# Causal masks moved to TensorE and probability sums shared by two engines in a two-layer attention kernel

## Chip, cores and metric

The kernel runs on one core of a Trainium2 chip. The metric is the device time of one execution in microseconds (us), smaller is better. The engines have short names in the profile: PE is TensorE (matmuls), PEld its weight loads, DVE VectorE, ACT ScalarE, POOL GpSimd, SP SyncE (here it only issues DMAs).

## The reference

The program is two transformer layers over 2048 tokens of width 512. Layer 0 is linear attention plus a mixture of 16 experts, layer 1 is softmax attention in a causal window of 1024 tokens (16 heads of 32) plus a block on the 256 tokens that a router picks. The change touches one piece of layer 1 alone, the softmax attention:

```python
scores = jnp.einsum('bhqd,bhkd->bhqk', q, k) / np.sqrt(HD)
scores = jnp.where(mask[None, None, :, :], scores, NEG)
attn = jax.nn.softmax(scores, axis=-1)
out = jnp.einsum('bhqk,bhkd->bhqd', attn, v)
```

with `mask = (q_idx >= k_idx) & (q_idx - k_idx <= 1024)` over n = 2048 tokens. A query sees itself and the 1024 tokens ahead of it, so in tiles of 128 tokens a query tile needs at most nine key tiles. The first of the nine (the edge of the window) and the last (the diagonal) are half masked.

## The kernel before

**Two passes over the scores.** The kernel computes the scores twice. The first pass (`maxima`, line 498) has queries on the partitions and finds the largest score of each query and head; it adds its masks on PE, as matmuls of a bf16 identity with a bf16 mask (`ident_b`, `mask_b`, lines 520 to 526). The negated maxima are kept transposed in `negT`, in two bf16 halves. This pass runs piece by piece between other work and ends at about 1462 us.

The second pass is the last stage of the program, from line 1054 on. It has the keys on the partitions, so that the exponentials can go into the next matmul without a transpose. It goes by *groups* (Q, g): Q is a block of four query tiles (512 queries), g a set of four heads. Each group goes by *units* (`units`, line 1077). A unit is one key tile against the query tiles of the block that see it. Key tiles seen by all four query tiles make whole units. Those at the edge of the window see only the first one, two or three query tiles, and are joined with the diagonal ones, which see the rest, so that such a unit has two key tiles and is full too. Q 0 has four units, the last three of them shorter (384, 256 and 128 queries); Q 1 has eight, the last three short in the same way; Q 2 and Q 3 have nine full ones. The order of the groups is written out in lines 1230 and 1231: (2,0), (0,0), (2,1), (0,1) and so on to (0,3), then (1,0) to (1,3), then (3,0) to (3,3).

**What a unit does.** `probabilities` (line 1093) takes two tiles of score buffers in PSUM from `ps_s` (three buffers, each two heads by 512 queries). PE writes the scores of the four heads side by side, each in its own 32 rows of the array (line 1104), and adds the negated maxima with a matmul over two rows (line 1111). Where the unit touches the edge or the diagonal, VectorE adds the mask `maskT` in PSUM (line 1128), once for each half (two heads). ScalarE then takes the exponential of each half (line 1137) into SBUF. The first unit of a group writes its exponentials into `acc`, the accumulator of the group; the others write to `pt`, a ring of six buffers, that is three units.

**Values and sums.** One step later PE multiplies the probabilities by the values (`values`, line 1169; the matmul is line 1177) into the PSUM tile `av`. The softmax also needs the sum of the probabilities over all keys. `gathered` (line 1197) does this in one of two ways. Either PE multiplies the unit's probabilities by a block of ones into the PSUM tile `sm` (`sums`, line 1186; matmul in line 1191), or the unit is added elementwise to `acc` (line 1210), by GpSimd, or, for unit 2 of the groups with Q > 0, by VectorE. `summed` (line 1162) chooses: PE takes the full units with even number except 0 and 2. There is one `sm` tile only, for all groups in turn.

**The end of a group.** `ending` (line 1212) is a generator of which one piece is run after each step of the next group. Its first piece only waits. The second has PE sum `acc` into `sm`, and VectorE take the reciprocal of two of its four blocks of 128 queries (line 1219) and multiply the values in `aT` by it (line 1220). The third does the other two blocks. With the last set of heads (g = 3) four pieces follow, each of which multiplies one query tile by `w_out` and adds the residual (`output`, line 1141). What is left of an ending when the next group is over is run at once.

**The loop** (line 1233) emits, for each unit: its scores, mask and exponential; then values and sums of the unit before; then one piece of the ending. Each engine works through its own queue in that order and waits by semaphores where it needs another one's result or a free buffer.

Of the kernel before, what the change touches and what calls it, by code (L numbers as in the profile page):

```python
# [19 lines left out]
P = 128  # L20
# [18 lines left out]
def two_layer_kernel(ctx: ExitStack, tc: tile.TileContext, a: dict, out: bass.AP):  # L39
# [6 lines left out]
    def const(shape, name, pool=cpool, dtype=F32):  # L46
        return pool.tile(shape, dtype, tag=name, name=name)
# [55 lines left out]
    def vcopy(o, i):  # L103
        V.tensor_copy(o, i)
# [354 lines left out]

    mask = const([P, 3, P], "mask", l1)  # L460
    maskT = const([P, 2, P], "maskT", l1)
    mask_b = const([P, 3, P], "mask_b", l1, BF16)
    for m in (mask, maskT):
        G.memset(m, 0.0)
    for m, step, mult in (
# [4 lines left out]
            channel_multiplier=mult,  # L470
        )
    vcopy(mask_b, mask)
    ones_b = const([P, P], "ones_b", l1, BF16)
    G.memset(ones_b, 1.0)
    ones_f = const([P, HD], "ones_f", l1)
# [590 lines left out]
        )  # L1066
    w_out = const([P, NC, D], "w_out", vo_pool)
    load(nc.sync, w_out, a["w_out"].rearrange("(c p) o -> p c o", p=P))
    pt = ctx.enter_context(tc.tile_pool(name="pt", bufs=6, reuse_waits="tile"))
    acc_pool = ctx.enter_context(tc.tile_pool(name="acc_pool", bufs=2, reuse_waits="tile"))  # L1070
    wk = ctx.enter_context(tc.tile_pool(name="wk7", bufs=2, reuse_waits="tile"))
    ps_s = ctx.enter_context(tc.tile_pool(name="ps_s", bufs=3, **tight))
# [20 lines left out]
    def probabilities(g, unit, name, base):  # L1093


        q0, q1 = unit[0][1] * P, (unit[-1][2] + 1) * P
        n = q1 - q0
        pS = [
            ps_s.tile([P, 2, QT * P], F32, tag="s", name=f"ps_{name}_{hp}") for hp in range(2)
        ]  # L1100
        for m, (kb, t0, t1) in enumerate(unit):
            for h in range(4):
                r = slice(h * HD, (h + 1) * HD)
                PE.matmul(  # L1104
                    pS[h // 2][:, h % 2, t0 * P - q0 : (t1 + 1) * P - q0],
                    kT[r, g, kb * P : (kb + 1) * P], qT[r, g, t0 * P : (t1 + 1) * P],
                    start=m == 0, stop=False, skip_group_check=True,
                )
        for h in range(4):
            r = slice(h * HD, h * HD + 2)  # L1110
            PE.matmul(  # L1111
                pS[h // 2][:, h % 2, :n], ones_b[r, :], negT[r, g, q0:q1], start=False, stop=True,
                skip_group_check=True,
            )
        edge = unit[0][2] == unit[0][0] + NWB - 1
        causal = unit[-1][1] == unit[-1][0]
        spots = []
        if edge and causal and len(unit) == 2:
            spots = [(unit[0][2], 0, 2)]
        else:  # L1120
            spots += [(unit[0][2], 0, 1)] if edge else []
            spots += [(unit[-1][1], 1, 2)] if causal else []
        got = []
        for hp in range(2):
            for tile_, m0, m1 in spots:
                s = slice(tile_ * P - q0, tile_ * P - q0 + (m1 - m0) * P)
                w = (m1 - m0) * P
                V.tensor_tensor(  # L1128
                    pS[hp][:, :, s], pS[hp][:, :, s],
                    maskT[:, m0:m1, :].rearrange("p m k -> p (m k)").unsqueeze(1)  # L1130
                    .to_broadcast([P, 2, w]), ALU.add,
                )
            if base:
                pT = acc_pool.tile([P, 2, QT * P], F32, tag=f"acc{hp}", name=f"acc_{name}_{hp}")
            else:
                pT = pt.tile([P, 2, QT * P], F32, tag="pt", name=f"pt_{name}_{hp}")
            S.activation(pT[:, :, :n], pS[hp][:, :, :n], AF.Exp)  # L1137
            got.append(pT)
        return got
# [14 lines left out]
    class Group:  # L1154
# [7 lines left out]
        def summed(self, n):  # L1162


            if (self.Q, self.g) == (NT // QT - 1, NC - 1) and n == len(self.us) - 2:
                return True
            return n % 2 == 0 and n != 2 and self.us[n][-1][2] - self.us[n][0][1] == QT - 1

        def values(self, n, got):
            Q, g, unit = self.Q, self.g, self.us[n]  # L1170
# [26 lines left out]
        def gathered(self, n, got):  # L1197

            unit, o = self.us[n], QT * self.Q * P
            q0, q1 = unit[0][1] * P - o, (unit[-1][2] + 1) * P - o  # L1200
            if n == 0:
                self.acc = got
            elif self.summed(n):
                self.sums(got, q0, q1, False)
            else:

                eng = V if n == 2 and self.Q > 0 else G
                for hp in range(2):
                    part = self.acc[hp][:, :, q0:q1]
                    eng.tensor_tensor(part, part, got[hp][:, :, : q1 - q0], ALU.add)  # L1210

        def ending(self):

            Q, g, aT = self.Q, self.g, self.aT
            yield
            self.sums(self.acc, 0, QT * P, True)
            for j in range(QT):
                js = slice(j * P, (j + 1) * P)
                V.reciprocal(self.sm[:, js], self.sm[:, js])  # L1219
                V.tensor_tensor(aT[:, g, js], aT[:, g, js], self.sm[:, js], ALU.mult)  # L1220
                if j % 2:
                    yield
            if g == NC - 1:
                for j in range(QT):
                    output(QT * Q + j, aT, j * P)
                    yield
# [79 lines left out]
```

## Time and profile before

| what | value |
|---|---|
| median of three timed runs | 1873.57 us (1873.55 to 1880.08) |
| the profiled execution, its own time | 1869.43 us |
| its span, from the first instruction to the last | 1867.7 us |
| granted TensorE clock, mean | 0.970 of full speed |
| second score pass, first score matmul to last sum | 1463.3 to 1849.9 us |
| score steps in it | 120, 72 of them with a mask |
| mask adds on VectorE (line 1128) | 144, 68.3 us busy |
| adds to acc (line 1210) | 126 on GpSimd, 253.8 us; 24 on VectorE |
| exponentials (line 1137) | 240, of which 208 to pt: 182.2 us |
| matmuls of sums (line 1191) | 360, of which 232 for single units |

A row of the page's fifth part, or of an answer by line, names the line, engine and operation, what it writes and reads with its shape, how often, the busy time, the mean of one in ns, and the idle time of the engine just ahead of it with what ended it. A float32 matmul shows as two instructions, so one unit of four heads shows as eight. In a table of windows the columns are start and end, length, the busy time and number of instructions of PE, PEld, DVE, ACT and POOL, then the granted clock, the DMA share and GB/s. A line of a timeline has the start in us, the time to the end of the last of a run of like instructions, engine, line, operation and number; in brackets the idle time ahead of it. Matmuls are pipelined, so how long a piece of PE's work takes is read from the start of one run of matmuls to the start of the next, not from the ends.

### The profile page before, as it was taken

The page shows a single profiled execution, that of the slowest core. Times are in us where ns is not written, and L with a number is a line of the kernel's source. Part 1 is how long each engine was busy: PE and PEld are TensorE (multiplying, and loading weights), DVE is VectorE, ACT ScalarE, POOL GpSimd, SP SyncE. Part 2 cuts the span into 40 slices and gives each one's busy share as a digit, 9 for nine tenths or more (in the row PEclk, how much of TensorE's full clock was granted, in tenths as well). Part 3 has the DMA queues.
Part 4 walks back from the last instruction along what each step waited for, and adds up shares of the span by engine and source line. Part 5 has one row for each costly group of instructions (what it writes and reads, how often), then busy time and mean ns, then how long its engine had stood idle before and what let it go on. Part 6 is the DMA issues. An engine that isn't in the chain of part 4 may idle for free. (4 is left out here: it accounts for less than half of the span.)

```text
span 1867.7 us, 20604 instructions
## 1 busy us (share of the span) xinstructions
PE 1740.5 (93%) x8120; PEld 767.4 (41%) x8120; DVE 1008.1 (54%) x1445; ACT 573.7 (31%) x923; POOL 497.2 (27%) x372
## 2 busy tenths in 40 slices
PE   7999999999999999868988887999999999999999
PEld 4555444344444333323433333454565333333333
DVE  6775645436445343696666564575555455444344
ACT  3212334233233243111111111142100366446463
POOL 2110000100100110333344431331000467458583
PEclk9999999999999999989999897999999899999999
DMA  9301001210213130100001004311132300110100
GB/s 362 128 29 43 23 28 39 85 34 29 72 53 74 33 109 23 62 23 23 23 23 29 26 12 149 122 51 68 46 111 92 91 1 1 35 57 1 46 1 35
DMA packets 61810, 107.12 MB, mean 57 GB/s; under 512 B 12209, under 2 KB 13745, under 8 KB 61201
## 3 DMA queue, kind: packets, MB, share of 16 engines
q1 hardware_dynamic: 55280, 104.01, 16.7%
q0 software_dynamic: 1152, 1.21, 0.4%
q8 instruction: 63, 1.03, 0.2%
q10 hardware_dynamic: 5280, 0.59, 0.2%
q14 instruction: 35, 0.28, 0.0%
HBM read 84.14 MB, written 21.65 MB: 57 GB/s over the span
## 5 line engine op out<-in xcount | busy, mean ns | idle before, releaser
L527 DVE TENSOR_REDUCE mx<-pa 128x4 f32<-128x1536 f32 (+3 forms) x144 | 252.9, 1756 | 178.2 <-PE pa L523 83.8
L1210 POOL TENSOR_TENSOR acc<-acc,pt 128x1024 f32<-128x1024 f32 (+3 forms) x126 | 253.8, 2047 | 122.1 <-ACT pt L1137 75.8
L1137 ACT ACTIVATE pt<-ps 128x1024 f32<-128x1024 f32 (+3 forms) x208 | 182.2, 923 | 138.1 <-DVE ps L1128 86.4
L515 PE MATMUL pa<-kT,qT 32*128 32x384 f32 (+3 forms) x1152 | 158.0, 562 | 47.5 <-DVE mx L527 39.3
L1104 PE MATMUL ps<-qT,kT 32*128 32x512 f32 (+3 forms) x1152 | 162.0, 535 | 8.6 <-ACT pt L1137 8.1
L93 POOL TENSOR_TENSOR xr<-xr,xn 128x512 f32<-128x512 f32 x16 | 27.0, 1697 | 493.6 <-DVE xn L87 493.6
L424 PE MATMUL acc<-h,rw2T 128*128 128x512 f32 x256 | 135.3, 616 | 14.9 <-DVE h L290 14.3
L288 ACT ACTIVATE r_e<-eg 128x512 f32<-128x512 f32 x128 | 75.8, 594 | 222.4 <-PE eg L419 202.4
L782 PE MATMUL p<-w_qk,xnt 128*128 128x512 f32 x256 | 129.7, 631 | 8.3 <-ACT xnt L107 8.3
L290 DVE TENSOR_TENSOR h<-ea,r_e 128x512 f32<-128x512 f32 x128 | 87.0, 686 | 87.2 <-ACT r_e L289 59.9
L421 PE MATMUL ea<-xw,rw1T 128*128 128x512 f32 x256 | 130.7, 592 | 0.0
L419 PE MATMUL eg<-xl,rwgT 128*128 128x512 f32 x256 | 130.7, 592 | 0.0
L1128 DVE TENSOR_TENSOR ps<-ps,maskT 128x256 f32<-128x256 f32 (+1 forms) x144 | 68.3, 514 | 100.3 <-PE ps L1111 97.2
L1104 PEld LDWEIGHTS ps<-qT,kT 32*128 32x128 f32 x1152 | 62.2, 186 | 116.5 <-issue 55.4
L515 PEld LDWEIGHTS pa<-kT,qT 32*128 32x128 f32 x1152 | 52.0, 191 | 138.3 <-DVE mx L527 88.0
L1177 PE MATMUL av<-pt,v 128*32 128x512 f32 (+3 forms) x1024 | 102.3, 485 | 0.2
L415 DVE TENSOR_TENSOR xw<-xw,xl 128x512 f32<-128x512 f32 x64 | 43.9, 685 | 94.9 <-DMA xw<-w_d 94.9
L1219 DVE RECIPROCAL sm<-sm 128x128 f32<-128x128 f32 x64 | 61.8, 965 | 57.4 <-PE sm L1191 56.0
L424 PEld LDWEIGHTS acc<-h,rw2T 128*128 128x128 f32 x256 | 43.4, 188 | 95.5 <-DVE h L290 79.4
L289 ACT ACTIVATE r_e<-r_e 128x512 f32<-128x512 f32 x128 | 80.2, 629 | 6.4 <-issue 1.9
L650 POOL TENSOR_TENSOR t<-qk,cosg 128x1024 f32<-128x1024 f32 x15 | 35.3, 2354 | 161.7 <-DVE qk L645 145.5
L421 PEld LDWEIGHTS ea<-xw,rw1T 128*128 128x128 f32 x256 | 48.6, 190 | 61.2 <-issue 60.8
(278 smaller groups left out, 2542.2 us busy)
## 6 DMA issues: line engine op xcount, KB each, us to landing
xw<-w_d SPq DMA_DIRECT2D x64, 256.0 KB, 3.2
x<-in_x SPq DMA_DIRECT2D x16, 256.0 KB, 4.3
res_d<-x SPq DMA_DIRECT2D x16, 256.0 KB, 2.3
xr<-res_d SPq DMA_DIRECT2D x16, 256.0 KB, 4.8
xn_d<-xn SPq DMA_DIRECT2D x16, 256.0 KB, 2.4
res_d<-xr SPq DMA_DIRECT2D x16, 256.0 KB, 2.0
xnq<-xn_d SPq DMA_DIRECT2D x16, 256.0 KB, 2.9
v_d<-vt SPq DMA_DIRECT2D x16, 256.0 KB, 2.9
```

Source lines behind the costliest of these rows:

```text
L289: S.activation(r, r, AF.Square)
L290: V.tensor_tensor(dst, pa, r, ALU.mult)
L419: PE.matmul(pg, rwgT[:, e, hb], xl, start=True, stop=True)
L421: PE.matmul(pa, rw1T[:, e, hb], xw, start=True, stop=True)
L424: PE.matmul(acc, rw2T[:, j, e, :], h, start=e == 0 and j == 0, stop=e == E - 1 and j == 1,)
L515: PE.matmul(pS[:, h, : w * P], qT[r, g, i * P : (i + 1) * P], kT[r, g, ks], start=True, stop=not (edge or last),)
L527: V.tensor_reduce(mx[:, g, :, c], pS[:, :, : w * P], AX.X, ALU.max)
L782: PE.matmul(pj, xnt[:, c, :], w, start=c == 0, stop=c == NC - 1)
L1104: PE.matmul(pS[h // 2][:, h % 2, t0 * P - q0 : (t1 + 1) * P - q0], kT[r, g, kb * P : (kb + 1) * P], qT[r, g, t0 * P : (t1 + 1) * P], start ...
L1137: S.activation(pT[:, :, :n], pS[hp][:, :, :n], AF.Exp)
L1177: PE.matmul(self.av[h * HD : (h + 1) * HD, t0 * P - o : (t1 + 1) * P - o], vs[kb // 4][:, kb % 4, hs], got[h // 2][:, h % 2, t0 * P - q0 : ...
L1210: eng.tensor_tensor(part, part, got[hp][:, :, : q1 - q0], ALU.add)
```

## The change

Three things change, all in the second pass.

The masks of this pass are added by PE: a bf16 copy `maskT_b` of `maskT` is made once, and after the matmul of the negated maxima four matmuls per masked unit, one for each head, add `ident_b` times the mask into the scores. VectorE's 144 adds in PSUM are gone. A mask matmul has 128 columns where one mask applies, 256 where the unit joins edge and diagonal.

Of each group at most one unit is summed on PE (13 in all, 29 before): none for Q 0, unit 4 for Q 1, the last unit for Q 2 and Q 3, and as before also the last but one of the very last group. All other units are added to `acc`, the odd ones by GpSimd and the even ones by VectorE: 110 adds on GpSimd and 72 on VectorE.

The `pt` ring has eight buffers instead of six, and for groups with Q > 0 the ending begins after three idle pieces instead of one, so that the sums of `acc` are emitted in the fourth step of the next group. What is left of it when a Q 0 group is over (the second half of the divisions, and for (2,3) all four outputs) is emitted in one run in the first step of the group after.

The order of the instructions of ScalarE and SyncE is the same as before. On PE, VectorE and GpSimd nothing differs ahead of this pass except the one cast that makes `maskT_b`.

```diff
--- before.py
+++ after.py
@@ -459,6 +459,7 @@
 
     mask = const([P, 3, P], "mask", l1)
     maskT = const([P, 2, P], "maskT", l1)
+    maskT_b = const([P, 2, P], "maskT_b", l1, BF16)
     mask_b = const([P, 3, P], "mask_b", l1, BF16)
     for m in (mask, maskT):
         G.memset(m, 0.0)
@@ -470,6 +471,7 @@
             channel_multiplier=mult,
         )
     vcopy(mask_b, mask)
+    vcopy(maskT_b, maskT)
     ones_b = const([P, P], "ones_b", l1, BF16)
     G.memset(ones_b, 1.0)
     ones_f = const([P, HD], "ones_f", l1)
@@ -1066,7 +1068,7 @@
         )
     w_out = const([P, NC, D], "w_out", vo_pool)
     load(nc.sync, w_out, a["w_out"].rearrange("(c p) o -> p c o", p=P))
-    pt = ctx.enter_context(tc.tile_pool(name="pt", bufs=6, reuse_waits="tile"))
+    pt = ctx.enter_context(tc.tile_pool(name="pt", bufs=8, reuse_waits="tile"))
     acc_pool = ctx.enter_context(tc.tile_pool(name="acc_pool", bufs=2, reuse_waits="tile"))
     wk = ctx.enter_context(tc.tile_pool(name="wk7", bufs=2, reuse_waits="tile"))
     ps_s = ctx.enter_context(tc.tile_pool(name="ps_s", bufs=3, **tight))
@@ -1106,12 +1108,6 @@
                     kT[r, g, kb * P : (kb + 1) * P], qT[r, g, t0 * P : (t1 + 1) * P],
                     start=m == 0, stop=False, skip_group_check=True,
                 )
-        for h in range(4):
-            r = slice(h * HD, h * HD + 2)
-            PE.matmul(
-                pS[h // 2][:, h % 2, :n], ones_b[r, :], negT[r, g, q0:q1], start=False, stop=True,
-                skip_group_check=True,
-            )
         edge = unit[0][2] == unit[0][0] + NWB - 1
         causal = unit[-1][1] == unit[-1][0]
         spots = []
@@ -1120,16 +1116,23 @@
         else:
             spots += [(unit[0][2], 0, 1)] if edge else []
             spots += [(unit[-1][1], 1, 2)] if causal else []
+        for h in range(4):
+            r = slice(h * HD, h * HD + 2)
+            PE.matmul(
+                pS[h // 2][:, h % 2, :n], ones_b[r, :], negT[r, g, q0:q1], start=False,
+                stop=not spots, skip_group_check=True,
+            )
+
+        for m, (tile_, m0, m1) in enumerate(spots):
+            s = slice(tile_ * P - q0, tile_ * P - q0 + (m1 - m0) * P)
+            for h in range(4):
+                PE.matmul(
+                    pS[h // 2][:, h % 2, s], ident_b,
+                    maskT_b[:, m0:m1, :].rearrange("p m k -> p (m k)"), start=False,
+                    stop=m == len(spots) - 1, skip_group_check=True,
+                )
         got = []
         for hp in range(2):
-            for tile_, m0, m1 in spots:
-                s = slice(tile_ * P - q0, tile_ * P - q0 + (m1 - m0) * P)
-                w = (m1 - m0) * P
-                V.tensor_tensor(
-                    pS[hp][:, :, s], pS[hp][:, :, s],
-                    maskT[:, m0:m1, :].rearrange("p m k -> p (m k)").unsqueeze(1)
-                    .to_broadcast([P, 2, w]), ALU.add,
-                )
             if base:
                 pT = acc_pool.tile([P, 2, QT * P], F32, tag=f"acc{hp}", name=f"acc_{name}_{hp}")
             else:
@@ -1164,7 +1167,7 @@
 
             if (self.Q, self.g) == (NT // QT - 1, NC - 1) and n == len(self.us) - 2:
                 return True
-            return n % 2 == 0 and n != 2 and self.us[n][-1][2] - self.us[n][0][1] == QT - 1
+            return n == {0: -1, 1: 4}.get(self.Q, len(self.us) - 1)
 
         def values(self, n, got):
             Q, g, unit = self.Q, self.g, self.us[n]
@@ -1204,7 +1207,7 @@
                 self.sums(got, q0, q1, False)
             else:
 
-                eng = V if n == 2 and self.Q > 0 else G
+                eng = G if n % 2 else V
                 for hp in range(2):
                     part = self.acc[hp][:, :, q0:q1]
                     eng.tensor_tensor(part, part, got[hp][:, :, : q1 - q0], ALU.add)
@@ -1212,7 +1215,8 @@
         def ending(self):
 
             Q, g, aT = self.Q, self.g, self.aT
-            yield
+            for _ in range(3 if Q > 0 else 1):
+                yield
             self.sums(self.acc, 0, QT * P, True)
             for j in range(QT):
                 js = slice(j * P, (j + 1) * P)
```

## The prediction

> **What bounds the kernel now.** I read the page first, then the table of windows for the second score pass (first score matmul at 1463.3 us, last probability sum at 1849.9 us), then TensorE's timeline inside it, then the groups of line 1210, at last the waits.
>
> ```profile
> PE 1740.5 (93%) x8120; PEld 767.4 (41%) x8120; DVE 1008.1 (54%) x1445; ACT 573.7 (31%) x923; POOL 497.2 (27%) x372
> L1128 DVE TENSOR_TENSOR ps<-ps,maskT 128x256 f32<-128x256 f32 (+1 forms) x144 | 68.3, 514 | 100.3 <-PE ps L1111 97.2
> ...
> 1463.00:1850.00 387.00, 377.90 (x3245) 132.15 (x3246) 175.87 (x301) 220.91 (x257) 255.42 (x127) 0.97 0.09 28
> ```
>
> In the pass PE is busy 377.9 of 387 us, VectorE 175.9, ScalarE 220.9, GpSimd 255.4. But a "busy" PE may be one whose matmuls are stretched by a wait, so I go by the starts:
>
> ```profile
> 1436.36 0.40 PE L523 MATMUL pa<-mask_b,ident_b 128*128 128x128 bf16 x4
> 1436.59 1.08 PE L1035 MATMUL pm<-wd,act 128*128 128x512 f32 x2
> ...
> 1772.94 1.14 PE L1104 MATMUL ps<-qT,kT 32*128 32x512 f32 x8
> 1773.90 0.40 PE L1111 MATMUL ps<-negT,ones_b 2*128 2x512 bf16 x4
> 1774.23 1.07 PE L1177 MATMUL av<-pt,v 128*32 128x512 f32 x8
> 1775.23 1.36 PE L1104 MATMUL ps<-qT,kT 32*128 32x512 f32 x8
> ...
> 1781.53 1.07 PE L1177 MATMUL av<-pt,v 128*32 128x512 f32 x8
> 1782.41 1.04 PE L1191 MATMUL sm<-pt,ones_f 128*32 128x512 f32 x8
> 1783.38 1.15 PE L1104 MATMUL ps<-qT,kT 32*128 32x128 f32 x16
> ```
>
> A step without a wait is 0.96 (scores) + 0.33 (maxima) + 1.00 (values) = 2.29 us. A unit summed on PE makes it 0.85 longer (values and sums take 1.85 here, 1781.53 to 1783.38). Four mask matmuls of 128 columns in the first pass cost 0.23 (1436.36 to 1436.59).
>
> The pair of groups (Q 2, then Q 0) from 1503.28 to 1540.54 took 37.26 us. Its floor: nine steps of 2.29 for Q 2, for Q 0 by the same reading 2.29, 1.84, 1.33 and 0.86, and five sums: 20.6 + 6.3 + 4.25 = 31.2. So PE waits 6.1 us in a pair, mostly where VectorE's mask stands between scores and exponential. A Q 3 group takes 26.4 us, 2.5 of them waits; a Q 1 group 20.6 in the mean of three.
>
> Last, who adds probabilities:
>
> ```profile
> L1210 POOL TENSOR_TENSOR acc<-acc,pt x126: 724/2356/3426, 1471.5 to 1840.4; 128x1024 f32<-128x1024 f32 x78, 128x768 f32<-128x768 f32 x16, 128x512 f32<-128x512 f32 x16, 128x256 f32<-128x256 f32 x16
> L1210 DVE TENSOR_TENSOR acc<-acc,pt x24: 1206/1215/2232, 1475.0 to 1832.4; 128x1024 f32<-128x1024 f32 x24
> ...
> 1799.60 0.97 DVE L1219 RECIPROCAL sm<-sm 128x128 f32<-128x128 f32 x1 [4.39 <-PE sm L1191]
> 1801.00 0.97 DVE L1219 RECIPROCAL sm<-sm 128x128 f32<-128x128 f32 x1
> ```
>
> A GpSimd add takes 2.36 us, a VectorE add 1.21, but the longest are 3.43 and 2.23: each time the two met, the later one was longer by what was left of the other. The recip and multiply of one 128-column block take 1.33, four of them 5.3 us.
>
> [...] the masks (one operand in PSUM) ran beside GpSimd without loss, 0.70 at most. [...] The trace is divided: values followed by sums take 0.88, followed by scores 1.00, so about 0.11 for a change; scores followed by full-array masks in the first pass show none (1435.50 to 1436.36 is two passes of 0.43).
>
> **The change part by part.** Against the profiled execution: span 1867.7, its own time 1869.4, which is 0.2% under the 1873.6 median.
>
> *PE.* Of the 29 units summed on PE 13 stay: 16 x 0.85 = 13.6 us less. Masks: 48 units get four matmuls of 128 columns at 0.23 = 11.0; 24 get four of 256. No row shows these[...]. PE gets 8.0 us more work. Bounds: [...] nothing comes off, since the matmuls must run.
>
> *VectorE.* 144 masks go (68.3 us), 48 adds come: 72 instead of 24, of them 32 more of 1.21 and 16 of half the elements, estimated at 0.65, 49 us in all. Its sum falls little; its place changes: no mask is left between scores and exponential. What then sets PE's waits is the score buffer (three, two used per unit): the exponential of the first half ends 0.16 + 0.97 us after the scores, and PE has 1.00 of values to do meanwhile, so 0.1 a step remains, and 0.64 after the first step of Q 2 or Q 1, whose values are short. The one cast of the mask (about 0.3 us, near 775 us) lies in front of a 1.6 us idle stretch of VectorE: nothing.
>
> *A pair for PE alone.* 26.9 + 3 x 0.85 + masks (two of 0.23, three of 0.44, four of 0.23 in Q 0: 2.7) + 0.64 + 0.3 = 33.1 instead of 37.26.
>
> *The new wait.* The sums of a group now come three steps into the next, and both groups share the one PSUM tile sm. Q 0's sums (second step of the next Q 2) wait until VectorE has divided Q 2's; those divisions stand in its queue behind the add of Q 0's unit 2; that waits for GpSimd's unit 1; that for the end of Q 2's chain of adds, in which every link now is serial[...]. Round the loop, from one pair's Q 0 sums to the next: sums 0.97 + start 0.1 + divisions 5.3, then V, G, V, G, V, G for units 2 to 7 (V pair 2.2, from 1476.12 to 1478.33[...]; G pair 4.6) 20.4, G of unit 1 of Q 0 with 768 elements 3.55, V 1.2, divisions 5.3: 36.8 us. Longer than PE's 33.1, so the pair takes 36.8. The first pair (40.0 before, at a lower clock) has no divisions in front and saves 4.1. Its chain starts 8.2 in, where GpSimd's first add is now: 8.2 + 4.6 + 20.4 + 3.55 + 1.2 + 5.3 = 43.2, and PE asks for sm at 35.9 + 4.7 = 40.6. It waits 2.6, so the second pair saves 1.5, the other two 0.5 each: 6.6.
>
> *The outputs of Q 2* now go out in one run at the start of Q 1, behind the same divisions. Counted from the last pair's start, without its wait, V ends at 36.1 and the first block is divided at 37.4; PE is there at 33.1 + 1.9 = 35.0 and waits 2.4. Q 1's first group, whose waits are hidden under outputs now, has 0.9 of masks: together -3.3.
>
> *Q 1, groups 1 to 3.* PE alone 19.0 (15.5 of steps, two sums, 0.9 masks, 0.9 waits). Unit 4's sums need sm, whose divisions stand behind V of unit 2, and that behind G of unit 1. From the group's start: unit 1's first half is ready at 4.9, + 0.1 + 4.6 + 2.2 + 5.3 = 17.1; PE is there at 14.9 (six steps of 1.9, 2.9, 2.35, 3.2, 2.35 and 2.2). So 21.2 instead of 20.6: -1.8.
>
> *Q 3.* PE: 20.6 + two sums 1.7 + masks 1.8 + waits 0.2 = 24.3. The chain of adds takes 4 x 4.6 + 3 x 2.2 + 0.7 (V of unit 4 behind divisions) = 25.7, but its sum is wanted 10 us into the next group only, so for three groups PE's time counts. Saved: 0.9 (first, 25.2 without its outputs), 2.05 and 2.2. In the last one the chain starts 2.8 late and nothing follows that hides it: its sums wait 2.4, and 0.6 is left of 3.0. Together +5.75.
>
> Sum: 6.6 - 3.3 - 1.8 + 5.75 = 7.2 us, 0.4%. The buffers (eight) carry a chain that is up to four units late; with six, ScalarE would wait.
>
> **Rivals.** *The chain doesn't bind* (divisions start earlier, adds overlap more): PE alone sets the time. Then 4 x 4.1 - 0.9 + 3 x 1.6 + 8.15 = 28.4: 1845. For it: PE is 93% busy, and GpSimd's adds stood 75.8 us waiting for exponentials, which then come sooner. Against: the loop's links are all measured.
> *Every change of hands costs more.* GpSimd and VectorE will hand the accumulator over six times in a Q 2 or Q 3 group, where it is twice in the kernel before, so the trace shows few handovers, and no loss in them. The loop has nine such links. At 0.5 us each a pair takes 41.3: the third and fourth pairs then lose 4 each, the second 1.4, the outputs behind 2.5 more, each Q 1 group 1.0 more, and in Q 3 the chain (29.4) sets the pace: -5.3 - 5.8 - 4.8 - 6 = -22. In between it goes in a line: it turns the gain into a loss from 0.13, a measurable one from 0.29. At 0.3 it is -10: 1884.
> *The masks on PE cost more than 0.23 and 0.44* moves the forecast by up to 7.9, less where the loop hides it.
>
> **How the numbers follow.** What tells from no change is about 0.5%, 9.4 us. Forecast 0.45: 1873.6 - 7.2 = 1866 (1862.2 in the profiled execution), own range 1858 to 1875. Chain not binding 0.33, handovers 0.22. Faster: 0.33 and the forecast's lower edge 0.07 = 0.40; slower: most of the handover case, 0.20; the rest 0.40. The range for 8 in 10 takes in both rivals' centres: 1846 to 1885.
>
> **What would show it.** Right: waits of PE's sums for VectorE's multiply of 2 to 4 us at each Q 2 after the first and each Q 1 after the first; VectorE adds with a mean near 2 us[...]; pairs of some 36.8 us. Wrong: pairs near 33 us (first rival), GpSimd pairs much over 4.7 us with idle gaps at each handover (second), or mask matmuls that take more than 0.44 for four.

## The result, and the profile after

The changed kernel takes 1862.1 us in the median of 19 runs (1855.7 to 1870.8), the kernel before 1873.6 beside it on the same chip (1868.9 to 1880.1): a ratio of 0.9943, 95% interval 0.9930 to 0.9957, so by the ratio 10.7 us less (8.1 to 13.1; the two medians are 11.4 apart). The profiled execution spans 1853.8 us.

From the page of the kernel after, the engines' totals and the groups of the additions and exponentials (busy us, mean ns of one, idle us just before them and what ended most of it); then, from the table of windows, the second score pass (engines in the order PE, PEld, DVE, ACT, POOL, then the granted clock, the DMA share and GB/s):

```profile
PE 1728.1 (93%) x8280; PEld 772.6 (42%) x8280; DVE 1039.0 (56%) x1350; ACT 572.5 (31%) x923; POOL 490.7 (26%) x356
...
L1213 POOL TENSOR_TENSOR acc<-acc,pt 128x1024 f32<-128x1024 f32 (+2 forms) x110 | 246.8, 2267 | 125.8 <-ACT pt L1140 62.6
L1140 ACT ACTIVATE pt<-ps 128x1024 f32<-128x1024 f32 (+3 forms) x208 | 181.1, 923 | 131.4 <-PE ps L1129 74.2
...
L1213 DVE TENSOR_TENSOR acc<-acc,pt 128x1024 f32<-128x1024 f32 (+1 forms) x72 | 124.6, 1760 | 129.1 <-POOL acc L1213 104.3
```

```profile
1456.00:1836.00 380.00, 369.30 (x3405) 137.91 (x3405) 204.77 (x205) 219.87 (x257) 248.38 (x111) 0.98 0.09 29
```

The row of masks on VectorE is gone, and the exponentials now wait for PE's mask matmuls (L1129). VectorE's 72 additions take 124.6 us, where alone they would cost some 79 (56 of 1.21 us and 16 of 0.68, what those of each shape take that wait for nothing; the 49 of the prediction are for the 48 that come): their mean is 1.76 us, and 104.3 us of VectorE's idle time ended with a GpSimd addition. VectorE and GpSimd work on one chain, one after the other.

The second score pass, from the start of the first score matmul to the start of the last probability sum, is 386.1 us before and 379.0 after. The groups of the two profiles, each from the start of its first exponential to that of the next group's, worked out from the traces, with three of the experiments below beside them:

| Stretch | before | masks alone | change | Q 0 on GpSimd | + Q 1's sums early |
|---|---|---|---|---|---|
| first pair (Q 2 and Q 0) | 39.5 | 38.3 | 36.8 | 36.7 | 36.8 |
| second pair | 37.3 | 36.3 | 35.7 | 35.1 | 35.1 |
| third pair | 37.3 | 36.1 | 36.6 | 35.1 | 35.1 |
| fourth Q 2 | 26.3 | 26.1 | 28.2 | 25.2 | 25.2 |
| fourth Q 0, and Q 1's first group with outputs | 60.3 | 57.2 | 57.1 | 57.1 | 57.1 |
| Q 1, three groups | 61.8 | 60.7 | 66.5 | 68.1 | 59.1 |
| Q 3, first group with outputs | 40.2 | 41.2 | 38.9 | 38.9 | 38.7 |
| Q 3, the other three | 80.9 | 81.9 | 77.0 | 77.0 | 77.0 |

So the change gains 3.0 us in the pairs (the fourth Q 2 with them), 3.2 around the outputs of Q 2 and 5.3 in Q 3, and loses 4.7 in Q 1; with 0.3 ahead of the first exponential that is the 7.1 in all. The fourth Q 0, which the forecast counts with the pairs, stands with the outputs here. The pass starts 6.9 us earlier as well, in code that the change hardly touches.

TensorE's timeline of the change shows the price of a mask. The columns are start, length of the group, engine, line, output and inputs, tile, shape and count:

```profile
1776.29 1.15 PE L1106 MATMUL ps<-qT,kT 32*128 32x256 f32 x16
1777.26 0.40 PE L1121 MATMUL ps<-negT,ones_b 2*128 2x512 bf16 x4
1777.59 0.61 PE L1129 MATMUL ps<-maskT_b,ident_b 128*128 128x256 bf16 x4
1778.13 1.07 PE L1180 MATMUL av<-pt,v 128*32 128x128 f32 x16
...
1781.98 1.14 PE L1106 MATMUL ps<-qT,kT 32*128 32x512 f32 x8
1782.94 0.40 PE L1121 MATMUL ps<-negT,ones_b 2*128 2x512 bf16 x4
1783.27 0.40 PE L1129 MATMUL ps<-maskT_b,ident_b 128*128 128x128 bf16 x4
1783.60 1.07 PE L1180 MATMUL av<-pt,v 128*32 128x384 f32 x16
```

By the starts, four masks of 256 columns take 0.54 us (1777.59 to 1778.13) and four of 128 columns 0.33 (1783.27 to 1783.60). With 48 units of the one and 24 of the other, 48 x 0.33 + 24 x 0.54 = 28.8 us.

The new wait is there too. From TensorE's, VectorE's and GpSimd's timelines of the change, around the sums of the second Q 0 group (idle time and releaser in brackets):

```profile
1533.60 1.06 PE L1180 MATMUL av<-acc,v 128*32 128x512 f32 x8
1536.64 1.07 PE L1194 MATMUL sm<-acc,ones_f 128*32 128x512 f32 x8 [1.98 <-DVE aT L1224]
```

```profile
1510.83 4.50 DVE L1213 TENSOR_TENSOR acc<-acc,pt 128x1024 f32<-128x1024 f32 x2 [2.25 <-POOL acc L1213]
1517.58 4.50 DVE L1213 TENSOR_TENSOR acc<-acc,pt 128x1024 f32<-128x1024 f32 x2 [2.25 <-POOL acc L1213]
1528.44 2.89 DVE L1213 TENSOR_TENSOR acc<-acc,pt 128x512 f32<-128x512 f32 x2 [6.35 <-POOL acc L1213]
1531.25 0.95 DVE L1223 RECIPROCAL sm<-sm 128x128 f32<-128x128 f32 x1
```

```profile
1514.33 5.54 POOL L1213 TENSOR_TENSOR acc<-acc,pt 128x1024 f32<-128x1024 f32 x2 [1.23 <-DVE acc L1213]
1521.10 9.09 POOL L1213 TENSOR_TENSOR acc<-acc,pt 128x1024 f32<-128x1024 f32 x4 [1.23 <-DVE acc L1213]
```

The sums of Q 2 were finished at 1529.52, where the next scores start; VectorE was held by the addition of Q 0's unit 2, which waited 6.35 us for GpSimd, and took up its first division at 1531.25. With 0.88 us for the values ahead of them, the sums could have started at 1534.5; they start at 1536.64. The two VectorE pairs are 6.75 us apart: one link of each engine, no more than the 4.6 + 2.2 read from the kernel before, so nothing is lost at the change of hands.

### The profile page after: what moved, and what is told of

Read it like the earlier page. It is cut to its first block, busy times and chain, and to the rows that moved or that the text cites. A ratio compares the mean times of both kernels' runs of the same rounds, so it can differ in the third digit from the quotient of the medians.

```text
span 1853.8 us, 20783 instructions
## 1 busy us (share of the span) xinstructions
PE 1728.1 (93%) x8280; PEld 772.6 (42%) x8280; DVE 1039.0 (56%) x1350; ACT 572.5 (31%) x923; POOL 490.7 (26%) x356
## 3 DMA queue, kind: packets, MB, share of 16 engines
q1 hardware_dynamic: 55280, 104.01, 17.1%
q0 software_dynamic: 1152, 1.21, 0.4%
## 5 line engine op out<-in xcount | busy, mean ns | idle before, releaser
L1213 POOL TENSOR_TENSOR acc<-acc,pt 128x1024 f32<-128x1024 f32 (+2 forms) x110 | 246.8, 2267 | 125.8 <-ACT pt L1140 62.6
L1213 DVE TENSOR_TENSOR acc<-acc,pt 128x1024 f32<-128x1024 f32 (+1 forms) x72 | 124.6, 1760 | 129.1 <-POOL acc L1213 104.3
L1106 PE MATMUL ps<-qT,kT 32*128 32x512 f32 (+3 forms) x1152 | 142.0, 537 | 0.0
L1106 PEld LDWEIGHTS ps<-qT,kT 32*128 32x128 f32 x1152 | 55.1, 187 | 94.8 <-issue 68.5
L419 PEld LDWEIGHTS eg<-xl,rwgT 128*128 128x128 f32 x256 | 48.6, 190 | 61.2 <-issue 60.0
```

Of the source, the lines that this page charges most:

```text
L419: PE.matmul(pg, rwgT[:, e, hb], xl, start=True, stop=True)
L1106: PE.matmul(pS[h // 2][:, h % 2, t0 * P - q0 : (t1 + 1) * P - q0], kT[r, g, kb * P : (kb + 1) * P], qT[r, g, t0 * P : (t1 + 1) * P], start ...
```

## The experiments

Each ratio is to the kernel before on the same chip; "the pass" is measured as above.

**Masks alone.** The change without its new rules for units and for the end of a group, and with six probability buffers.

```
-            return n == {0: -1, 1: 4}.get(self.Q, len(self.us) - 1)
+            return n % 2 == 0 and n != 2 and self.us[n][-1][2] - self.us[n][0][1] == QT - 1
...
-                eng = G if n % 2 else V
+                eng = V if n == 2 and self.Q > 0 else G
...
-            for _ in range(3 if Q > 0 else 1):
-                yield
+            yield
```

> The masks of the change alone (added by PE); probability sums, ring of six buffers and ending as in the kernel before. Theory 1 (what pays is that VectorE no longer stands between scores and exponential): PE gets 28.8 us of mask matmuls (0.33 and 0.54 per unit, as the trace after shows), but its waits of some 6 us in a pair, 3 in a Q 1 group and 2.5 in a Q 3 group fall to about 1, 1 and 0.3. A pair takes 35.7 instead of 37.3, Q 1 groups 19.4, Q 3 groups 26.5: 5 to 11 us faster than before in all, so about as fast as the whole change. Theory 2 (the time was saved by taking 16 units off PE's sums): PE is 98% busy in the pass, so 28.8 us of added matmuls make it 15 to 29 us slower than before.

Measured: 1865.1 us, ratio 0.9961 (0.9948 to 0.9974), pass 380.3. So the masks alone bring 5.8 of the pass's 7.1 us. By the runs alone the change can't be told from them: the intervals of 0.9961 and 0.9943 overlap.

By estimate the clock has a large part in these 5.8 us. The first 10.2 us or so of the pass run at half the clock in every kernel here: from 1460 to 1480 the mean is 0.74 in all but the change, whose pass starts earlier (0.50 from 1457.0 to 1467.2). Beyond them the kernel before has another 10.2 us at half the clock, masks alone has none. From the table of windows of TensorE, first before, then masks alone (window, length, PE busy, clock, DMA share, GB/s):

```profile
1613.90:1620.70 6.80, 6.72 (x20) 0.50 0.01 2
1689.00:1692.40 3.40, 3.40 (x20) 0.50 0.00 0
```

```profile
1474.00:1841.00 367.00, 366.66 (x3450) 1.00 0.08 26
```

If half the clock costs half of the time, as an estimate, that is up to 5.1 of the 5.8 us. What PE gains by shorter waits is then nearly used up by the 28.8 us of mask matmuls. Whether the clock stayed up because those waits are gone, no run shows by itself; the last section has what points to it.

The table above shows where the other half of the change works: against masks alone it gains 7.2 us in Q 3, and gives back 5.8 in Q 1 and 0.3 in the pairs and outputs.

**The sums alone.** The kernel before with the new rules and eight probability buffers, the masks still on VectorE.

```
-            return n % 2 == 0 and n != 2 and self.us[n][-1][2] - self.us[n][0][1] == QT - 1
+            return n == {0: -1, 1: 4}.get(self.Q, len(self.us) - 1)
...
-                eng = V if n == 2 and self.Q > 0 else G
+                eng = G if n % 2 else V
```

> The other half alone: fewer units summed on PE, GpSimd and VectorE in turns, eight buffers, ending three steps later; the masks stay on VectorE. Theory 1: the masks now queue behind VectorE adds[...] and behind an accumulator that is late, so exponentials and PE wait for them: 20 to 45 us slower than before. Theory 2: 16 x 0.85 = 13.6 us of matmuls are gone, 8 to 14 us faster than before.

Measured: 1953.7 us, ratio 1.0424 (1.0381 to 1.0468), pass 469.9. The sign was right, the size was not. From the timeline of this kernel, in a Q 3 group:

```profile
1841.47 4.50 DVE L1210 TENSOR_TENSOR acc<-acc,pt 128x1024 f32<-128x1024 f32 x2 [5.87 <-POOL acc L1210]
...
1850.73 1.21 DVE L1210 TENSOR_TENSOR acc<-acc,pt 128x1024 f32<-128x1024 f32 x1
1851.85 0.27 DVE L1221 TENSOR_TENSOR aT<-aT,sm 128x128 f32<-128x128 f32 x1
1852.04 1.22 DVE L1210 TENSOR_TENSOR acc<-acc,pt 128x1024 f32<-128x1024 f32 x1
1853.18 0.75 DVE L1128 TENSOR_TENSOR ps<-ps,maskT 128x256 f32<-128x256 f32 x2
1853.69 1.94 ACT L1137 ACTIVATE pt<-ps 128x1024 f32<-128x1024 f32 x2 [5.80 <-DVE ps L1128]
...
1854.77 2.08 PE L1104 MATMUL ps<-qT,kT 32*128 32x128 f32 x12 [4.98 <-ACT pt L1137]
```

The mask stands late in VectorE's queue: the addition at 1841.47 had waited 5.87 us for GpSimd, and the divisions and the next addition, which stand behind it, come before the mask. ScalarE waits 5.80 us for the mask, PE 4.98 for ScalarE's score buffer. The two halves of the change are not a sum: the masks had to leave VectorE before its queue could hold a chain. The table of windows shows a mean granted clock of 0.86 in this pass against 0.97 in that of the kernel before, which the 20 to 45 us of the expectation had not counted.

**The chain without VectorE.** The even units' additions are left out.

```
-            else:
+            elif n % 2:
...
-                eng = G if n % 2 else V
+                eng = G
```

> The change with VectorE's 72 adds left out (units of even number are not in the sums, a part of the computation is missing). Theory 1 (loop of divisions, VectorE and GpSimd adds, [...]one sm tile): GpSimd pairs are 4.7 us without waits, the divisions stand behind nothing, PE's nine waits for sm (11 us over the floor by the starts) go: 9 to 13 us faster than the whole change. Theory 3 (PE's own work sets the time[...]): within 2 us of the whole change.

Measured: 1854.1 us, ratio 0.9901 (0.9863 to 0.9940), pass 369.5, which is 9.5 us shorter than the change's. PE does the same work here; the even units are missing from the sums, and with them VectorE's links from the chain. So these 9.5 us are what PE loses to the chain with VectorE's links in it: 4.9 in the pairs and the fourth Q 2, 5.0 in Q 1, and nothing in Q 3. Even so the pass is only 386.1 - 369.5 = 16.6 us shorter than that of the kernel before, where the prediction's first rival, with PE alone setting the time, has 28.4.

**Sums two pieces later instead of three.**

```
-            for _ in range(3 if Q > 0 else 1):
+            for _ in range(2 if Q > 0 else 1):
```

> The change with the ending begun after two idle pieces instead of three. Then the first half of the divisions stands ahead of VectorE's add of unit 2 and only the second half behind it. Theory 1: sm is free 2.6 us earlier, PE waits for it at most 1 us in Q 1 (now 2.0) and 0 to 1 in Q 2 (now 1.2 to 2.2); in Q 3 PE may wait 0.5 for the accumulator: 3 to 7 us faster than the whole change. Theory 3: within 2 us of it, or slower by what PE then waits for the accumulator.

A miss: 1868.1 us, ratio 0.9964 (0.9950 to 0.9979), pass 383.0, 4.0 longer than the change's. I had taken it that the divisions would come ahead of VectorE's next addition. They don't; from this kernel's timeline of VectorE:

```profile
1539.70 2.89 DVE L1213 TENSOR_TENSOR acc<-acc,pt 128x512 f32<-128x512 f32 x2 [6.35 <-POOL acc L1213]
1542.52 0.95 DVE L1223 RECIPROCAL sm<-sm 128x128 f32<-128x128 f32 x1
```

The addition still comes first and waits the same 6.35 us. In the kernel's text the first half of the divisions now stands ahead of it, so VectorE's queue does not keep the order of the text everywhere; what sets its order, no run shows. In Q 1 the sums stand before an sm that is free no earlier, with waits of 1.98 us where the change has 1.77, and all three groups take 23.2 us, where two of the change's take 21.7. Half-clock stretches go with that difference: in Q 1 one of the change's three waits is followed by 3.4 us at half the clock, and that group takes 23.2 us too; here all three waits are. From the table of windows of TensorE (a window of 20 us with one such stretch has a mean near 0.92):

```profile
1680.00:1700.00 20.00, 19.91 (x183) 0.92 0.01 2
1700.00:1720.00 20.00, 17.98 (x164) 0.91 0.00 1
1720.00:1740.00 20.00, 17.97 (x172) 0.91 0.01 2
```

Asking a step sooner did not shorten a wait here.

**The cast and the ring alone.** The kernel before with the bf16 mask and eight probability buffers, for the question whether the 6.9 us ahead of the pass belong to the change.

```
+    maskT_b = const([P, 2, P], "maskT_b", l1, BF16)
...
+    vcopy(maskT_b, maskT)
...
-    pt = ctx.enter_context(tc.tile_pool(name="pt", bufs=6, reuse_waits="tile"))
+    pt = ctx.enter_context(tc.tile_pool(name="pt", bufs=8, reuse_waits="tile"))
```

> The kernel before with only the bf16 copy of the mask and eight instead of six probability buffers. Theory 1 (all of the gain arises inside the second score pass, from masks and chain; the 6.9 us by which the two profiles differ ahead of the pass are run-to-run variation): no change, ratio 0.998 to 1.002, pass 386 to 388 us. Rival (the copy shifts the work ahead of the pass, or the deeper ring alone frees ScalarE): 3 to 8 us faster than the kernel before.

Measured: 1873.2 us, ratio 1.0009 (0.9997 to 1.0020). They bring nothing. The pass starts at 1468.4 us here and at 1456.4 in the change, whose code ahead of the pass is the same, so its start varies by as much as 12 us with the execution, and the 6.9 us need be no effect of the change. The pass itself is 389.3 us long, 3.2 more than in the profile of the kernel before, and the windows say why: the groups 1573.6 to 1616.1 ran at a lower granted clock (columns: window, length, PE busy, clock, DMA share, GB/s).

```profile
1573.63:1586.39 12.76, 11.33 (x114) 0.81 0.01 1
1586.39:1616.13 29.74, 29.46 (x248) 0.85 0.00 1
```

**Six buffers.** The change with six probability buffers, as many as before.

```
-    pt = ctx.enter_context(tc.tile_pool(name="pt", bufs=8, reuse_waits="tile"))
+    pt = ctx.enter_context(tc.tile_pool(name="pt", bufs=6, reuse_waits="tile"))
```

> The full change with six probability buffers instead of eight. Theory 1 (the chain of additions runs up to four units late, so that it holds eight half-unit buffers): ScalarE waits for a free buffer and PE behind it; 5 to 20 us slower than the full change, so about no gain or a loss against the kernel before. Rival (the chain is late, but six buffers carry it): within 2 us of the full change.

Measured: 1862.9 us, ratio 0.9944 (0.9915 to 0.9973), pass 379.1. The rival was right: six are enough. ScalarE's wait for a free buffer is 8.6 us in six places in the table of waits, and none of it shows in the length of the pass.

**Q 0's third unit on GpSimd.** So that no addition that waits stands ahead of Q 2's divisions.

```
-                eng = G if n % 2 else V
+                eng = V if n % 2 == 0 and self.Q > 0 else G
```

> The full change, but the third unit of each Q 0 group is added by GpSimd, so that the divisions of Q 2 do not stand behind a VectorE addition that waits for GpSimd. Theory 1 (the wait of 1.2 to 2.2 us before the sums of Q 0 comes from that place in VectorE's queue): the wait falls under 0.7 us at all three places, pairs of 34.5 to 35.5 us instead of 35.7 to 37.5, pass of 375 to 377 instead of 379.5 us, 2 to 5 us faster than the full change. Rival (GpSimd is the real limit of the loop: its two additions of 512 elements last 2.4 us where VectorE's last 1.2): the wait only moves from the divided block to the accumulator, pairs as long or up to 1.2 us longer, 0 to 4 us slower than the full change.

Measured: 1860.6 us, ratio 0.9935 (0.9912 to 0.9959), which by itself can't be told from the change's ratio. The profile can: pass 375.4 us, pairs of 35.1, and these lines of TensorE's and VectorE's timelines.

```profile
1542.33 1.06 PE L1180 MATMUL av<-acc,v 128*32 128x512 f32 x8
1543.85 1.06 PE L1194 MATMUL sm<-acc,ones_f 128*32 128x512 f32 x8 [0.46 <-DVE aT L1224]
```

```profile
1538.38 0.97 DVE L1223 RECIPROCAL sm<-sm 128x128 f32<-128x128 f32 x1 [7.57 <-PE sm L1194]
```

VectorE now stands ready when the sums come, and PE's wait is 0.46 us instead of 1.98. Theory 1 holds for Q 2 and Q 0.

**Masks ahead of the maxima.** The mask loop moved in front of the four matmuls with the maxima, the flags of the last matmul with it.

```
-        for h in range(4):
-            r = slice(h * HD, h * HD + 2)
-            PE.matmul(
...
-                stop=not spots, skip_group_check=True,
-            )
         for m, (tile_, m0, m1) in enumerate(spots):
...
-                    stop=m == len(spots) - 1, skip_group_check=True,
+                    stop=False, skip_group_check=True,
                 )
+        for h in range(4):
+            r = slice(h * HD, h * HD + 2)
+            PE.matmul(
...
+                stop=True, skip_group_check=True,
+            )
```

> The full change with the mask matmuls put between the scores and the maxima instead of after the maxima. Theory A (the extra 0.11 us of a group of mask matmuls[...]; from scores to full-array masks there is none, as in the first pass): four masks of 128 columns take 0.22 to 0.24 us, four of 256 take 0.43 to 0.45, the maxima stay at 0.33; PE has 7 us less to do, the pass is 3 to 6 us shorter than the 379.5 us of the full change. Theory B (every change of mode costs the same wherever it stands): what the masks lose the maxima gain (0.44 instead of 0.33), or the masks stay at 0.33 and 0.54; the pass stays within 1.5 us of the full change.

Both theories fell: 1873.7 us, ratio 1.0017 (1.0007 to 1.0028), pass 389.1, 10 us longer than the change's. From TensorE's timeline of this kernel, and below it that of the first pass in the kernel before:

```profile
1770.78 1.14 PE L1106 MATMUL ps<-qT,kT 32*128 32x512 f32 x8
1771.85 0.40 PE L1122 MATMUL ps<-maskT_b,ident_b 128*128 128x128 bf16 x4
1772.18 0.39 PE L1129 MATMUL ps<-negT,ones_b 2*128 2x512 bf16 x4
1772.50 1.07 PE L1179 MATMUL av<-pt,v 128*32 128x384 f32 x16
```

```profile
1435.50 0.93 PE L515 MATMUL pa<-kT,qT 32*128 32x384 f32 x8
1436.36 0.40 PE L523 MATMUL pa<-mask_b,ident_b 128*128 128x128 bf16 x4
```

The masks still take 0.33 (1771.85 to 1772.18) and the maxima 0.32, and the scores ahead of the masks take 1.07 instead of 0.96. So the step from 32-row scores to full-array masks costs 0.11 more than the step from scores to maxima. With 72 such steps that makes 7.9 of the 10 us, but it is not the whole account: steps of joined units in Q 3 get longer by another 0.1 to 0.2, and some of PE's waits for sm get shorter. These two were not followed further. The same price had been in the first pass all along. Its scores are 384 columns wide: by the ratio to 512 columns (0.43 a pass in the outputs, next section) two passes are some 0.32 each, as an estimate, and not 0.43, and 0.86 - 0.64 = 0.22 of that group lies in the step from 32-row scores to full-array masks. In the second pass of the change scores of 384 columns take 0.75 before maxima (the fences of the prediction have the 512-column case, 0.96):

```profile
1664.41 1.15 PE L1106 MATMUL ps<-qT,kT 32*128 32x384 f32 x8
1665.16 0.57 PE L1121 MATMUL ps<-negT,ones_b 2*128 2x384 bf16 x4
```

In this kernel they take 0.86 before masks.

**Q 1's sums one piece into the next group.** On top of the version with Q 0 on GpSimd.

```
-            for _ in range(3 if Q > 0 else 1):
+            for _ in range(3 if Q > 1 else 1):
```

> The full change, with the third unit of Q 0 added by GpSimd and the sums of a Q 1 group put one idle piece into the next group (as in the kernel before) instead of three, so that VectorE's queue holds the divisions of Q 1 ahead of its addition of unit 2, not behind it. Theory 1 (each wait for sm in Q 1 is the divisions standing behind an addition that waits for GpSimd): the waits of 2.0 us in three Q 1 groups go, what is left is at most 0.8 us for the accumulator; Q 1 groups of 20.0 to 20.7 instead of 21.7 us, pass of 371 to 373.5 instead of 375.4 us, 6 to 9 us faster than the full change. Rival (the chain of additions is what is late, wherever the sums are put): the wait moves to the accumulator, Q 1 groups stay at 21.5 us or more, no faster than the version with Q 0 on GpSimd alone.

Measured: 1846.5 us, ratio 0.9876 (0.9855 to 0.9896), pass 366.3. It beats both kernels. From the table of waits (us in total, times, longest):

```profile
PE sm L1194 <- DVE aT L1224: 1.4, 3, 0.5
...
PEld sm L1194 <- POOL acc L1213: 0.9, 3, 0.3
```

In the change the first of these rows stands at 10.3 us in six places, 2.0 at most. In this kernel's timeline VectorE's divisions begin at 1663.40, in the second group of Q 1, and its addition of unit 2 follows at 1668.31; with two pieces the addition had still come first. Q 1's groups take 19.7 us, less than the 20.0 expected: the wait for the accumulator is 0.3 us at most. The pass is 4.7 us under the expected range. Of that 3.0 go with the stretch at half the clock behind Q 1's first wait (last section); neither is there in this kernel. In the version with Q 0 on GpSimd that group took 24.7, the two others 21.7.

**More links on VectorE, no unit summed on PE.** On top of the last version, in Q 2 and Q 3.

```
-            return n == {0: -1, 1: 4}.get(self.Q, len(self.us) - 1)
+            return (self.Q, n) == (1, 4)
...
-                eng = V if n % 2 == 0 and self.Q > 0 else G
+                pool = (1, 2, 3) if self.Q == 0 else (1, 3, 5, 7) if self.Q == 1 else (1, 4)
+                eng = G if n in pool else V
```

> The same version, and in Q 2 and Q 3 no unit is summed on PE any more (but the one of the very last group); all go into the chain, of which GpSimd takes only units 1 and 4 and VectorE the rest. Theory 1 (a link costs 4.6 us on GpSimd and 2.4 on VectorE, so a Q 3 chain of two and six takes 23.6 us, less than PE's 24.3; PE alone sets the pace): PE has seven sums of 0.86 us less, Q 3 groups of 24.2 to 24.5 instead of 25.2 us, pairs near 34.3 instead of 35.1, pass 5 to 7 us shorter. Rival (VectorE then has 14 us of additions and 5.3 of divisions in one queue in which each waits for the one ahead): the divisions or the chain come late, sums wait for acc or sm, and the pass is 0 to 15 us longer.

Measured: 1840.8 us, ratio 0.9849 (0.9827 to 0.9872), the lowest median of this study, with an interval that overlaps the last version's; pass 360.7, Q 3 groups 24.4, pairs 34.4. Theory 1 holds: each of the three lengths is as it forecast. From its page:

```profile
L1214 POOL TENSOR_TENSOR acc<-acc,pt 128x1024 f32<-128x1024 f32 (+3 forms) x88 | 172.6, 1988 | 176.4 <-PE av L1180 95.5
...
L1214 DVE TENSOR_TENSOR acc<-acc,pt 128x1024 f32<-128x1024 f32 (+1 forms) x110 | 144.5, 1367 | 59.6 <-ACT pt L1140 32.3
```

With fewer changes of engine VectorE's mean addition falls from 1.76 to 1.37 us; its idle time now ends mostly with exponentials and no longer mostly with GpSimd.

## Why the prediction held, and where its terms were off

The forecast took 7.2 us off the pass, and the two profiled passes differ by 7.1. The mechanism was right: PE is the bound, and the serial chain holds it up at the sums, through the divisions. The agreement of the totals is luck. The sizes by stretch were off both ways, the outputs even in sign, and the errors cancel: pairs 6.6 forecast and 3.0 measured, outputs -3.3 and +3.2, Q 1 -1.8 and -4.7, Q 3 +5.75 and +5.3. The profile of the kernel before is also only one execution: with the cast-and-ring kernel in its place the difference is 10.3.

*A step of 2.29 and a sum of 0.85* held where PE doesn't wait.

*The masks on PE.* The term "0.23" and "0.44" measured 0.33 and 0.54: 28.8 us instead of 21.6. The 0.44 for four masks of 256 columns (24 x 0.44 = 10.6) was the author's estimate; no row of the kernel before shows it, and twice its row of 0.23 would be 0.46. What failed is the price taken from the first pass. The 0.23 was read where another full-array matmul follows the masks (the prediction's row at 1436.59), as it does everywhere in that pass. In the second pass the 32-column values follow, and the masks take 0.33. The maxima ahead of them stay at 0.33, so the added 0.10 us is on the way out of the masks. The reading that was to rule such a cost out, "scores followed by full-array masks in the first pass show none (1435.50 to 1436.36 is two passes of 0.43)", is wrong too: the row says 32x384 and was read as 512 columns. The upper bound that the prediction kept, 7.9 us, was near the truth (28.8 - 21.6 = 7.2). The runs put the step from masks to values at 0.10 us (0.33 against 0.23), and the step from scores to masks at 0.11 more than that from scores to maxima (1.07 against 0.96); what PE does in that time, no trace shows. In Q 3, where nothing hides it, five masked steps cost 0.5 of the 0.9 us by which a group (25.2) is longer than forecast (24.3).

*The pairs.* Loop and floor were forecast at 36.8 and 33.1. The floor was 2.0 too low: without VectorE's links, and with Q 0 on GpSimd, a pair takes 35.1. Of the 2.0, 0.9 are the nine mask groups; the rest are waits for score buffers and the 0.5 that the sums of Q 0 still wait. In Q 1 PE alone was put at 19.0 and takes 19.7, in Q 3 at 24.3 and takes 25.2. Links of 4.6 + 2.2 were measured as 6.75, the second and third pair as 35.7 and 36.6, and the waits for sm in Q 2 by the starts as 1.2, 2.2 and 2.2 (forecast 2 to 4). The first pair gained 2.7 instead of 4.1, and the fourth Q 2 lost 1.9 at a clock of 0.94 after its wait. That this wait is the divisions behind an addition, and not a loss at each change of hands, is shown by Q 0 on GpSimd: 0.46 us is left of it, with GpSimd and VectorE still taking turns in Q 2.

*The outputs of Q 2* were to wait 2.4 us and don't: 32 output matmuls run in 13.9, about 0.43 each, and the table of waits has 0.2 us for them. The step that failed is "PE is there at 33.1 + 1.9 = 35.0 and waits 2.4". The likely reason: an output adds up four groups, and only the last needs the block that is divided last; the three ahead of it give 6 x 0.43 = 2.6 us of cover. The 17.7 us of the fourth Q 0 in the kernel before had also been a stretch at a clock of 0.81 (6.8 us of it at half the clock, so by estimate up to 3.4 of the 17.7), which made the baseline longer than I took it for.

*Q 1* was to lose 1.8 us and lost 4.7. The groups that ran at full clock take 21.7 against the forecast 21.2; the first of the three took 23.2. Its waits for sm of 2.0 are as forecast (17.1 - 14.9 = 2.2).

*Q 3* was to gain 5.75 and gained 5.3: the masks took more, and the last group's sums wait 0.2 instead of 2.4, probably since PE's longer period keeps the chain in step.

*"With six, ScalarE would wait"*: it does, for 8.6 us, but the pass is no longer than the change's.

*The rivals.* That the chain doesn't bind, and that handovers cost 0.3 to 0.5 us each, are both refuted: the first by the chain without VectorE (9.5 us), the second by the 6.75 us of a pair of links.

The 10.7 us of the runs against 7.1 of the pass stay partly open. With the cast-and-ring kernel the difference is 389.3 - 379.0 = 10.3: its pass and that of the kernel before, with the same work in them, differ by 3.2 us, most of the 3.6 that are missing, and their stretches at half the clock lie partly at other places.

## What to carry to other kernels

Before moving work off an engine, ask which queue it stood in and what stood ahead of it there: the masks brought 5.8 us by leaving VectorE's queue, most of it, by estimate, time at half the clock that was no longer there, and most of the 7.2 us that the new chain gained in Q 3 went again because divisions that PE waits for stood behind additions that wait for GpSimd. When a wait is found, look at what the releasing engine did just before, and reorder that queue (9 us here, 3 of them beside a stretch at half the clock); asking one step sooner made the pass 4 us longer, and two more buffers did nothing. And take a price only from a row whose shape and whose neighbours are those of the new place: here a row of 384 columns was read as 512, and masks followed by full-array matmuls stood for masks followed by narrow ones.

## What the runs showed of the hardware

**Stretches at half the clock stood behind PE's short waits.** From the change's timeline and table of windows of TensorE, at the first wait for sm in Q 1:

```profile
1668.83 1.93 PE L1194 MATMUL sm<-pt,ones_f 128*32 128x512 f32 x8 [1.77 <-DVE aT L1224]
1670.69 1.24 PE L1106 MATMUL ps<-qT,kT 32*128 32x256 f32 x8
```

```profile
1660.00:1668.00 8.00, 7.05 (x66) 1.00 0.00 0
1668.00:1672.00 4.00, 3.17 (x20) 0.58 0.02 4
1672.00:1680.00 8.00, 7.95 (x88) 1.00 0.00 0
```

After 1.8 us of waiting the sums take 1.86 us (1668.83 to 1670.69) where they take 1.00 elsewhere, and the clock of those 4 us is 0.58. Such a dip stands beside the wait in two of the change's six places. In the five kernels with waits of 1.7 to 2.1 us before sums (the change, two pieces, six buffers, Q 0 on GpSimd, masks ahead of the maxima) 11 of 21 such waits were followed by 3.4 or 6.8 us at half the clock, and none of the three of 1.0 us. That is a strong sign, though not a proof: no run changed the clock alone, and the kernel before and its cast-and-ring version have such stretches at other places, which differ in part between the two. Masks alone and the two fastest versions, whose PE is idle for 0.3 of 381 us, 1.8 of 367 and 1.8 of 362, show no 20 us window under 0.98 in the pass after its start (1460 to 1480); the sums alone, with PE idle for 58 of 470 us, average 0.86. A wait counted at its own length was counted too low there: in Q 1's second group the version with Q 0 on GpSimd took 24.7 us, 3.0 more than the two groups after it with the same wait.

**Where VectorE's and GpSimd's additions met, the later one was longer.** VectorE's additions of 1024 elements went from 1.21 us alone to as much as 3.38 in the change, and the mean of all its 72 is 1.76; GpSimd's longest is 3.41 (3.43 before), against 2.36 alone. In the two traces the additions of the two engines overlap 69 times (13 before, 56 after), and each time the later one is longer by what is left of the earlier, less 0.07 to 0.15 us. At 1473.43 in the change, for one, 2.29 us of GpSimd's were left and VectorE's took 3.37. This part of the waiting stands in the page as length of an instruction and not as idle time. The kernel before's masks were not longer beside GpSimd's additions: the 41 of 512 elements that overlap one take 0.69 to 0.70 us, as the seven others do. None of the additions is longer than 1.21 + 2.36 = 3.57, the two one after the other; what the two engines share, the traces do not show.
